# Layer 0 of a four-layer network: k's transposes into free quarters of the scores' PSUM banks, the group norm's deviation on ScalarE, two pieces of side work at other steps

## Chip, core and metric

The kernel runs on one core of one Trainium2 chip, as one launch. The metric is device time in microseconds (us), the median of several executions. Engines are named as the profile names them: PE is TensorE's matrix multiply and PEld its weight load, DVE is VectorE, ACT is ScalarE, POOL is GpSimd, SP is SyncE, which here only issues DMAs. All arithmetic is fp32.

## The reference, cut to what matters

The input x is 16 images of 192 channels on 32 by 32 pixels. Four layers follow each other, each as `x = x + layer(group_norm(x))`, and every group norm has 32 groups, so 6 channels each:

```python
def _gn(v, G=32, eps=1e-5):
    g = v.reshape(B_, G, C_ // G, H_, W_)
    m = jnp.mean(g, axis=(2, 3, 4), keepdims=True)
    s = jnp.var(g, axis=(2, 3, 4), keepdims=True)
    return ((g - m) / jnp.sqrt(s + eps)).reshape(v.shape)
```

Layer 0, where nearly all of this case happens, normalises the 1024 tokens of an image over channels, projects them to 2 x 384 (`x_in`, `z`), puts `x_in` through a causal convolution of 4 taps and a silu (`x_act`), and makes q and k from it and v from `x_in`. A recurrence with 12 heads of 32 follows:

```python
C_new = f_s * Cst + i_s * (vt[..., :, None] * kt[..., None, :])
n_new = f_s * nst + i_s * kt
h = einsum('bhde,bhe->bhd', C_new, qt) / max(abs(einsum('bhd,bhd->bh', n_new, qt)), 1)
```

Its output is normalised per head, gated, projected down and added to the tokens; a silu branch (`w_lin`) is added; a dense 3 by 3 convolution over the image and a batch norm follow. Layer 1 and layer 3 are selective scans (16 states, 384 channels), layer 2 is a depthwise convolution with batch norm.

## The kernel before, in words

**Order.** The program is written as Python generators whose instructions a scheduler then puts in an order for each engine, once, before the launch. On the chip each engine runs its own list strictly in that order. So an instruction that waits holds up everything behind it on its engine. In layer 0 the products of the recurrence are also tied to each other in a fixed order on PE (`self.main`, a chain of order-only dependencies), and the other products fall between them.

**Layer 0.** The tokens are worked on in chunks of 128, so 8 chunks to an image and 128 in all (`layer0_step`, one step per chunk). The recurrence is done chunk-wise, as in linear attention. For chunk g one step does this:

- The e tile (128 x 12 x 128: the log weights between two tokens of the chunk, per head) comes by a DMA that spreads a row over all partitions (L700). POOL adds the mask and the second gate term to it (L705, L706; both over 128 x 1536), ACT takes the exponential (L711). There are two e tiles.
- PE makes the scores, 12 products of q and k (L722), into four PSUM tiles called s, one bank each. Each uses 3 x 128 of the bank's 512 columns.
- PE transposes the chunk of k (three products, L727) into a PSUM tile called mm and DVE copies it out as kt (L728). PE transposes the chunk of v (L733) into another mm, and ACT copies it out (L736).
- DVE multiplies scores by e into four tiles p (L753; three buffers for four tiles, so the fourth waits for the first product that uses the first). PE multiplies p by v (num, L779). PE adds what comes through the state (L767) and makes the new state from kt and vr (L806; vr is made by POOL, L755).
- The output of the chunk before is normalised (L827 to L841), transposed by PE into another mm (L851) and gated (L854, L857).

[...] four for s, one for the convolution (`conv`), one for `num`, and **two for mm**. All short-lived products of layer 0, those of the recurrence as well as those of the side work, take turns in these two mm tiles. A product that needs an mm tile waits on PE until an earlier one has been read out.

**Side work of layer 0.** A small scheduler in Python (`Side`) hands out the side work by step numbers with a start and an end. Four kinds are there: the image norm of the next image (`layer0_image`), the front of the next half image (`layer0_front`: layer norm, projections, convolution, silu, q, k, gates; 12 tiles of 512 tokens in some 2.7 steps), the spread of a finished image into the tiles ya and yb by way of DRAM (`layer0_spread`, L499 to L504), and the 3 by 3 convolution in three parts of 15 or 30 products (`layer0_conv2`, L520), which ends in a copy by ACT (L526) and batch-norm statistics by DVE (L528).

**The image norm** loads the image (L539, a single buffer), takes statistics on DVE (L351, L352), averages means over the groups by a product (L355), takes the deviation of the means (L357 to L362), averages that by a second product (L365), and needs 1/sqrt of it. Before, DVE adds eps (L367) and POOL raises to the power -0.5 (L309, `pow_mhalf`). DVE then scales the image (L543), and the front's first product (L377) reads it. `group_norm` is also used 48 times in layers 1, 2 and 3.

The layers 1 and 3 are scans. PE turns B x into place (L994, L997), ACT makes the decays (L986), DVE scans (L1010), POOL multiplies by C (L1017), PE sums the states (L1028).

## Time and profile before

| what | value |
|---|---|
| time before, median of 3 runs | 17368.59 us (17350.56 to 17390.61) |
| the profiled execution: its time, its span | 17403.5 us, 17401.7 us |
| granted TensorE clock over the span, mean | 0.951 |
| PE busy | 15749.6 us, 91% of the span |
| DVE, ACT, POOL busy | 75%, 68%, 66% |
| layer 0, from 120 to 3760 us: PE busy, granted clock | 3263.08 of 3640 us, 0.88 |
| layers 1 and 2, from 3944 to 7480 us: PE busy, granted clock | 3179.91 of 3536 us, 0.98 |
| layer 3, from 7800 to 17402 us: PE busy, granted clock | 8902.43 of 9602 us, 0.98 |

The profile is of one execution, and its span is measured from the first to the last instruction. A row of the waits names the engine, the line that waited, the line that released it, the total, the number of times and the longest. A row of the timeline gives start, length, engine, line, what is written from what, and in square brackets the idle time just before. PE shows two rows' counts for each fp32 product of the program. "PEclk" is the share of full speed that the clock of PE was granted. Where a wait has several causes the profile names the one that came last.

### The profile page before, as it was taken

The numbers are of one execution on the slowest core, as the hardware profiler recorded it, in microseconds if no ns is written. First come the engines' busy times: TensorE is split into PE (matmuls) and PEld (weight loads), VectorE is DVE, ScalarE is ACT, GpSimd is POOL, SyncE is SP. The second block draws the span as 40 slices with busy tenths as digits, with TensorE's granted clock in tenths as the row PEclk, the third lists the DMA queues.
The fourth block names the chain that finished last, engine by engine and source line by source line (L and its number), as shares of the span: only waits on it lengthen the run. The fifth ranks groups of instructions, "written<-read, shape, count | busy, mean of one in ns | idle before, by whom it ended". The sixth has DMA issues, their size and how long they took to land. (4 is left out here: it accounts for less than half of the span.)

```text
span 17401.7 us, 263068 instructions
## 1 busy us (share of the span) xinstructions
PE 15749.6 (91%) x99452; PEld 11013.2 (63%) x99452; DVE 13122.0 (75%) x14859; ACT 11873.6 (68%) x19637; POOL 11450.8 (66%) x5555
## 2 busy tenths in 40 slices
PE   8998988888988899979899999999999999999998
PEld 4444444435555555547777777777777777777777
DVE  4444444437777777749889888888888888888888
ACT  3222322327666666648888888888888888888888
POOL 3333333425555555538788788888878888888888
PEclk8889998989999999989999999999999999999999
DMA  1111111123333343433333333323333333333332
GB/s 51 42 40 44 44 43 44 47 63 107 114 110 110 113 118 116 118 99 103 90 99 107 93 96 101 107 83 99 107 98 92 99 108 88 96 105 102 88 98 67
DMA packets 890141, 1544.65 MB, mean 89 GB/s; under 512 B 83472, under 2 KB 314653, under 8 KB 879530
## 3 DMA queue, kind: packets, MB, share of 16 engines
q1 hardware_dynamic: 888874, 1527.81, 30.3%
q8 instruction: 788, 12.91, 0.3%
q14 instruction: 479, 3.92, 0.1%
HBM read 1284.22 MB, written 243.27 MB: 88 GB/s over the span
## 5 line engine op out<-in xcount | busy, mean ns | idle before, releaser
L1017 POOL TENSOR_TENSOR h<-h,cb 128x1536 f32<-128x1536 f32 x2560 | 8872.8, 3469 | 1432.0 <-DVE h L1010 902.9
L986 ACT ACTIVATE da<-dt,neg_a 128x512 f32<-128x512 f32 x7680 | 5267.0, 714 | 1752.0 <-DVE h L1010 1687.3
L1010 DVE TENSOR_TENSOR_SCAN h<-da,carry,xb 128x512 f32<-128x512 f32 x3840 | 4652.4, 1262 | 657.1 <-PE xb L997 596.2
L1028 PE MATMUL y<-const,h 128*128 128x128 f32 x30720 | 4717.9, 276 | 128.3 <-DVE ysum L1468 54.0
L1010 DVE TENSOR_TENSOR_SCAN h<-da,xb 128x512 f32<-128x512 f32 x3840 | 4440.6, 1202 | 388.7 <-PE xb L997 270.7
L994 PE MATMUL xb<-const,xbt 128*128 128x128 f32 x23040 | 4074.6, 282 | 422.5 <-DVE h L1010 269.3
L966 ACT ACTIVATE xbt<-ut,bt 128x384 f32<-128x384 f32 x7680 | 4174.4, 603 | 246.4 <-PE xb L994 244.3
L994 PEld LDWEIGHTS xb<-const,xbt 128*128 128x128 f32 x23040 | 2757.2, 143 | 1815.5 <-issue 643.8
L1028 PEld LDWEIGHTS y<-const,h 128*128 128x128 f32 x30720 | 3684.9, 143 | 322.8 <-issue 265.4
L997 PE MATMUL xb<-diag,ut 128*128 128x128 f32 x15360 | 3016.4, 279 | 0.0
L997 PEld LDWEIGHTS xb<-diag,ut 128*128 128x128 f32 x15360 | 2383.5, 195 | 63.1 <-issue 63.1
L830 POOL TENSOR_TENSOR hs<-h,mhm 128x384 f32<-128x384 f32 x128 | 108.5, 848 | 1685.1 <-DVE den L835 1290.5
L1016 POOL COPY carry<-h 128x3 f32<-128x3 f32 x1280 | 250.5, 196 | 1220.1 <-DVE h L1010 964.7
L976 POOL TENSOR_TENSOR diag<-const,bt 128x512 f32<-128x512 f32 x640 | 680.8, 1064 | 550.5 <-PE xb L997 362.1
L705 POOL TENSOR_TENSOR e<-e,const 128x1536 f32<-128x1536 f32 x128 | 439.9, 3437 | 288.9 <-DMA e<-row 273.0
L520 PE MATMUL conv<-ya,w_conv 128*64 128x512 f32 (+1 forms) x1152 | 543.9, 656 | 66.1 <-DMA ya<-yrows 62.2
L916 PE MATMUL mm<-dbl,w_dt 45*128 45x512 f32 x960 | 532.8, 639 | 33.6 <-DVE v L1490 16.2
L711 ACT ACTIVATE e<-e 128x1536 f32<-128x1536 f32 x128 | 189.7, 1482 | 417.7 <-POOL e L706 417.4
L854 DVE TENSOR_TENSOR ht<-sz,mm 128x384 f32<-128x384 f32 x128 | 70.7, 552 | 519.5 <-PE mm L851 519.5
L1171 PE MATMUL mm<-rep,t_dw 96*32 96x512 f32 x2304 | 433.5, 614 | 23.5 <-DMA rep<-xr 17.3
L779 PEld LDWEIGHTS num<-v,p 128*128 128x128 f32 x3072 | 389.3, 201 | 102.2 <-issue 77.9
L920 DVE SCALAR_TENSOR_TENSOR dt<-lnsq,mm 128x512 f32<-128x512 f32 x480 | 322.0, 671 | 171.9 <-ACT lnsq L919 171.9
(272 smaller groups left out, 17910.1 us busy)
## 6 DMA issues: line engine op xcount, KB each, us to landing
cb<-row SPq DMA_DIRECT2D x2560, 256.0 KB
rep<-xr SPq DMA_DIRECT2D x384, 331.0 KB
e<-row SPq DMA_DIRECT2D x128, 768.0 KB
rep<-xin SPq DMA_DIRECT2D x384, 256.0 KB
rep<-xr SPq DMA_DIRECT2D x384, 228.8 KB
x<-x SPq DMA_DIRECT2D x48, 768.0 KB
xr<-xin SPq DMA_DIRECT2D x48, 612.5 KB
xr<-xpad SPq DMA_DIRECT2D x32, 867.0 KB
```

What stands on the lines that cost most here:

```text
L520: nc.tensor.matmul(o, self.w_c2[:k, t, c0 : c0 + o.shape[0]], src[:k, r0 : r0 + 16, dx : dx + W], start=t == 0, stop=t == 14, skip_group_c ...
L705: nc.gpsimd.tensor_tensor(k.e, k.e, self.k0("mask")[:, None, :].to_broadcast([128, NH, 128]), ADD)
L916: nc.tensor.matmul(ps, w_dt[:, t * 128 : (t + 1) * 128], dbl, start=True, stop=True)
L966: nc.scalar.activation(t[:, c], u.ut[:, c], AF.Copy, scale=u.bt[:, c, n : n + 1])
L976: nc.gpsimd.tensor_tensor(d, ident[:, None, :].to_broadcast([128, 4, 128]), u.bt[:, 3, n : n + 4][:, :, None].to_broadcast([128, 4, 128]), ...
L986: nc.scalar.activation(da[i, t], u.dt[:, t], AF.Exp, scale=u.neg_a(t, n))
L994: in_order(nc.tensor.transpose(xb[i, t][:, c * 128 : (c + 1) * 128], xbt[i][:, c, t * 128 : (t + 1) * 128], ident))
L997: in_order(nc.tensor.matmul(xb[i, t][:, 384:], u.ut[:, 3, t * 128 : (t + 1) * 128], u.diag[n // 4][:, n % 4], start=True, stop=True, skip_ ...
L1010: nc.vector.tensor_tensor_scan(hv, dv, xv, 0.0 if first else u.carry_in[:, n, t : t + 1], MUL, ADD)
L1017: nc.gpsimd.tensor_tensor(h[i], h[i], u.c.pop(n)[:, None, :].to_broadcast([128, 3, 512]), MUL)
L1028: in_order(nc.tensor.matmul(u.y[:, j], h[i][:, t, c * 128 : (c + 1) * 128], ident, is_transpose=True, start=n == 0 and j % 4 == 0, stop=n ...
L1171: self.nc.tensor.matmul(ps[32 * g : 32 * g + 32], blocks[:, g * side + r], seen, start=r == 0, stop=r == side - 1, skip_group_check=True,)
```

## The change

- `group_norm`: eps is added and the power -0.5 is taken as `exp(-0.5 * ln(v + eps))` by two instructions of ACT. The instruction of DVE (L367) and that of POOL (L309) go. This holds for all 64 group norms.
- `layer0_scores`: the four s tiles become one tile of four banks with one buffer. The three transposes of k go to the fourth quarters of banks 0, 1 and 2 and no longer to an mm tile. One copy by DVE takes the three quarters out. The products, their number and shapes are the same.
- `layer0`: the image norm starts 1.1 steps earlier and ends 0.6 steps earlier; the convolution's parts start 0.3, 0.2 and 0.1 steps later, and end at the same step.

```diff
@@ group_norm
         r = pool.tile([HP, 2], F32, name="gnr")
-        nc.vector.tensor_scalar(r, ps[:HP, :2], EPS, None, ADD)
-        self.pow_mhalf(r)
+        nc.scalar.activation(r, ps[:HP, :2], AF.Ln, bias=self.k("eps", HP))
+        nc.scalar.activation(r, r, AF.Exp, scale=-0.5)
@@ layer0
             for b in range(1, self.nb):
-                side.add("image", self.layer0_image(b, sp, bp, psum), 8 * b - 5.1, 8 * b - 4)
+                side.add("image", self.layer0_image(b, sp, bp, psum), 8 * b - 6.2, 8 * b - 4.6)
...
                 for j in range(3):
-                    at = 8 * b + 9.6 + 2.4 * j
-                    side.add("conv", self.layer0_conv2(b, j, bp, psum), at, at + 2.4)
+                    at = 8 * b + 9.9 + 2.3 * j
+                    side.add("conv", self.layer0_conv2(b, j, bp, psum), at, at + 2.3)
@@ layer0_scores
-        k.s = [psum.tile([128, 3, 128], F32, name="s", bufs=4) for _ in range(4)]
+
+        banks = psum.tile([128, 4, 4, 128], F32, name="s", bufs=1)
+        k.s = [banks[:, j, :3] for j in range(4)]
...
         k.kt = bp.tile([128, DI], F32, name="kt")
-        ps = psum.tile([128, 512], F32, name="mm")
-        for t in range(3):
-            self.main(nc.tensor.transpose(ps[:, t * 128 : (t + 1) * 128], k_[:, t, k.tok], self.k("ident")))
-        nc.vector.tensor_copy(k.kt, ps[:, :DI])
+        for t in range(3):
+            self.main(nc.tensor.transpose(banks[:, t, 3], k_[:, t, k.tok], self.k("ident")))
+        nc.vector.tensor_copy(k.kt.rearrange("p (t d) -> p t d", t=3), banks[:, :3, 3])
```

## The prediction

> **What bounds the kernel now.** I read the busy slices first, then a table by stage, then PE's waits in layer 0, then the timeline around one image norm.

> ```profile
> 120.00:3760.00 3640.00, 3263.08 (x14031) 1656.52 (x14032) 1750.30 (x3516) 1071.99 (x1604) 1405.29 (x867) 0.88 0.17 43
> ```

> Columns: PE, PEld, DVE, ACT, POOL busy, then PE's clock. In layer 0 PE is busy for 3263 of 3640 us and no other engine reaches half. PE bounds it, with 377 us idle and a clock of 0.88. Layer 3 has 93% of PE at clock 0.98. The idle time by cause, same stretch (total, times, longest):

> ```profile
> PE mm L377 <- DVE x L543: 94.9, 14, 7.6
> PE mm L851 <- ACT v L736: 65.3, 23, 4.9
> PE conv L520 <- DMA ya<-yrows: 55.4, 15, 4.9
> PE mm L851 <- DVE kt L728: 44.5, 28, 3.5
> PE mm L733 <- DVE k L613: 19.4, 16, 2.1
> PE mm L607 <- ACT v L736: 16.0, 15, 1.3
> PE mm L365 <- ACT v L736: 15.2, 13, 1.6
> PE mm L733 <- DVE xn L389: 12.6, 19, 2.2
> PE mm L569 <- DVE kt L728: 12.5, 18, 1.3
> ```

> Three causes: the front waits for the normalised image (first row), the convolution for its tile (third), and all others for one of the two mm tiles. The timeline of one image norm:

> ```profile
> 2010.57 0.35 SPq L539 DMA_DIRECT2D x<-x  x1
> ...
> 2052.70 0.25 PE L355 MATMUL mm<-gnmv,const 96*96 96x2 f32 x2
> ...
> 2058.36 0.33 PE L365 MATMUL mm<-gnq,const 96*96 96x2 f32 x2 [1.61 <-ACT v L736]
> ...
> 2059.72 0.90 PE L851 MATMUL mm<-const,hs 128*128 128x128 f32 x3 [1.04 <-DVE kt L728]
> ...
> 2063.33 2.75 POOL L706 TENSOR_TENSOR e<-e,uw 128x1536 f32<-128x1536 f32 x1
> 2066.03 0.69 POOL L309 TENSOR_TENSOR gnr<-gnr,const 96x2 f32<-96x2 f32 x1
> ...
> 2069.90 3.73 PE L377 MATMUL mm<-x,const 96*96 96x512 f32 x4 [7.27 <-DVE x L543]
> ```

> The image is there at 2011, but its first product runs at 2052.70. The power then stands on POOL behind L705 and L706, until 2066, and PE stops for 7.27 us. This chunk loses 1.61 + 1.04 + 7.27 = 9.9 us.

> [...] L309 begins as L706 ends. [...] the trace has 1283 ns (L596, L598). [...] The trace shows clock 0.70 in the image chunk (2055.20 to 2083.90) against 0.92 in 2000 to 2044.

> **The change, part by part** (line numbers of before). I use the issue order that each program was built with.

> *Image norm and deviation.* SP's order around L539 is the same in both, and L539 already waits for POOL's L600 (the single image buffer), so the load comes no earlier. What moves is the rest. L355 now stands among k's projections, before the v transposes of chunk 3 (of 8), and L365 after that chunk's L851. ACT's Ln and Exp and DVE's L543 follow: a whole chunk before L377. The image's wait of 6.8 us (94.9/14) is gone with some 10 us to spare, and POOL loses 0.69 us per image.

> What is late next? In the image chunk DVE's order is now three of p, L854, L528, L379 twice, the fourth p, and L528 waits for ACT's L526, which stands behind the exponential of the *next* e (L711), hence behind POOL. POOL's L705 starts at 2059.83 (its row came by DMA), then L841 0.83, then L706 2.75: to 66.9; L711 1.48: 68.4; L526 0.67; L528 0.68; L379 1.28; p 0.55: about 71.6. The same work before:

> ```profile
> 2067.50 0.67 ACT L526 ACTIVATE y<-conv,p 128x512 f32<-128x512 f32 x1
> ...
> 2070.49 0.68 DVE L528 BATCH_NORM_STATS2 stats_a<-y 128x6 f32<-128x512 f32 x1
> ...
> 2077.06 0.56 DVE L753 TENSOR_TENSOR p<-s,e 128x384 f32<-128x384 f32 x1
> ...
> 2079.14 0.75 PE L779 MATMUL num<-v,p 128*128 128x33 f32 x6
> ```

> PE needs the fourth p (L753 here) for the last three num products. Before, these ran at 2079.14 with 9.9 us of stops; without stops PE would be there at 2069.2. So PE stops for about 2.4 us instead of 9.9: **7.5 us per image, 15 images: -113 us.** The next e row is fetched when p frees its tile, so the later chain shifts along.

> *k's transposes out of the mm tiles.* L851 no longer takes kt's tile. Of the 44.5 us of L851 behind L728, about 15 were counted above (1.04 per image), so **-29**. L569 behind kt, 12.5: **-7**, since it inherits part of the wait for xn. L733 waits 19.4 + 12.6 (+5.4 for L811) for a tile read out late; v now takes an older one. I take half: **-17**. The products cost the same (L727 has 304 ns, as the neighbours). The copy by DVE reads three runs in three banks: nearest row L854, also rearranged, 0.552 us against L728's 0.548. Its bounds are no change and twice that; DVE is 48% busy, and the copy now stands ahead of the p's, so even double is hidden except at the fourth p. [...] One tile of four banks is freed by the last reader, not one by one. That is the fourth p, which PE's chain needs ahead of the next scores anyhow: nothing.

> *What stays.* After an image, L851 of chunk 5 waits about 3.9 us for v, whose copy stands behind the next exponential on ACT. In the new order it still does so in 13 of 16 cases. The larger part of the 65.3 us stays: it gets 1 us longer as one convolution product ahead of it is gone, and 1.4 us shorter as POOL's chain is nearer. I take **-8**.

> *New small waits.* One convolution product no longer stands between chunk 6's v and q's projections (L607, which wait for v's copy): +1.0 x 16 = **+16**. L355 between k's projections takes a tile and makes the third projection wait for DVE's second read: about 1 x 14 = **+14**. ACT gets Ln and Exp, nearest rows L839 and L840 at 0.21 us; queued where ACT is mostly idle (busy 1.95 of 11 us, 2044 to 2055): nothing. Table loads: one more in the whole program, +1.3, before the first image.

> *Convolution.* In the built order the first product of an image (L520) stands where it stood, right behind v's transposes of chunk 2 and ahead of L607. The spread is unchanged on SP. So the 55.4 us **stay**; if the move worked they would go, the bound below. The other parts start about a dozen products later, as filler: nothing by themselves.

> *Clock.* L377 has 899 ns over its 120 rows where L589, of the same size, has 612: 34 us in the stage lost to the halved clock. With the stop before it gone I take about half, **-18**. Bounds: nothing, and -90 (a fifth of the 0.12 x 3640 = 437 us that the clock costs).

> *Layers 1 to 3.* In layer 3 PE's order is the same; in layers 1 and 2, 732 of 3474 products other than the scan's changed place by a few. PE's stops at the norm are 28.7 us (L377 behind L1240), 72.4 (L355 behind its statistics, which stays). DVE waits 23.7 us for POOL's power in layer 3, off PE's path. I take **-10**, between -60 and +60.

> Sum: -113 - 29 - 7 - 17 - 8 + 16 + 14 + 1 - 18 - 10 = **-171 us**. The profiled execution took 17403.5 and would come to 17232. It is 35 us above the median of the runs, 17368.6, which would come to **17198**.

> **The rivals.**

> *The fourth p gives half back* (0.20). If POOL's chain in the image chunk ends 4 us later than I worked out (the e row lands later, or DVE's L543, 0.8 to 4.7 us long, delays L694 and with it L706), the image is worth 3.5 us, not 7.5: 60 less, about 17260; up to 17330 if kt's waits return as well. For it: three engines in a row stand behind one DMA. Against: only L841 is put into that chain.

> *The clock recovers* (0.13): up to 90 instead of 18, or the convolution's 55 go too: 17060 to 17140. Against: a chunk that makes no image norm and idles 0.3 us (2172 to 2199) has clock 0.81, so short products alone lower it.

> *Nothing comes of it* (0.06): the stops move to other mm users, tile for tile, as the rows of L851 allow: 17334 to 17403.

> *The clock falls* (0.09, slower): convolution products, the long ones, leave the stretches between short products, and the halved clock spreads. Stage at 0.88 loses 437 us. To end 35 us slower it must lose 171 + 35 more, 643 of about 3675: clock 0.825. Below that point it decides; price about 17420. For it: 0.81 exists in this stage (2172 to 2199). Against: the number of long products per chunk changes by one or two[...].

> **How the numbers follow.** Likeliest, 17140 to 17250: 0.52. With the give-back, and most of the clock's recovery, 17100 to 17330 holds 8 in 10. A difference of 0.2%, 35 us, is about what a measurement of this kernel can tell. Faster by more: 0.52 + 0.20 + 0.13 = 0.85; within: 0.06; slower: 0.09.

> **What would show it.** Right: L377 behind L543 gone from PE's waits; L851 behind L728 gone; L520 behind ya still near 55; a new stop at num for p of 2 to 3 us per image; L607 behind v near 30; PE's idle time in layer 0 about 230 us instead of 377, the stage some 160 shorter; layers 1 to 3 within 60 us. Wrong: a stop of over 6 us at num per image (give-back), a clock in layer 0 under 0.85 (slower), or a difference that lies in layers 1 to 3.

## The result, and the profile after

The changed kernel takes **17154.22 us**, median of 4 runs (17148.25 to 17170.01), against 17367.28 us of the kernel before in the same comparison (17350.56 to 17390.61): a ratio of **0.9878, 95% interval 0.9861 to 0.9895**, 213 us less. On a second chip it was 17137.39 against 17360.18, 0.9875 (0.9859 to 0.9892). The prediction said 17198, between 17100 and 17330. The time is in the range. But only about a quarter of the gain is idle time of PE in layer 0, where the prediction looked for nearly all of it; the experiments below show where the rest came from.

The profiled execution took 17158.12 us, its span is 17156.3 us at a mean clock of 0.959 (before 0.951). Layer 0 ends some 190 us earlier: the first scan of layer 1 starts at 3755.3 us, before at 3943.8. Lines up to L717 keep their numbers; the scores, L722, are L724, and from L727 on every line is one higher (L736 is L737, L851 is L852).

The table by stage, for layer 0 of the kernel after, has the columns shown before the change (PE, PEld, DVE, ACT, POOL busy, then PE's clock):

```profile
120.00:3570.00 3450.00, 3127.78 (x14038) 1632.15 (x14039) 1751.20 (x3502) 1077.39 (x1638) 1403.58 (x852) 0.92 0.18 45
```

PE still idles 322 of 3450 us. That is 55 less than before, where the prediction expected some 147 less. The clock went from 0.88 to 0.92. PE's waits in layer 0 (total, times, longest):

```profile
PE mm L852 <- ACT v L737: 86.8, 24, 6.4
PE conv L520 <- DMA ya<-yrows: 61.2, 16, 6.4
PE conv L520 <- ACT y L526: 36.7, 12, 6.2
PE mm L569 <- DVE xn L389: 20.3, 13, 2.7
PE mm L607 <- ACT v L737: 18.1, 15, 1.3
PE num L780 <- DVE p L754: 17.2, 17, 2.2
...
PE mm L355 <- DVE k L613: 10.1, 13, 0.8
```

The rows of L377 behind L543 and of L851 behind kt are gone, as forecast, and the stop behind ya stayed. But L852 behind v grew from 65.3 to 86.8 us, and the row of the convolution that waits for its own bank until ACT has read it (L526) grew from 2.4 to 36.7. The timeline of one image norm shows both halves, the gain and the new stop:

```profile
1944.42 0.25 PE L365 MATMUL mm<-gnq,const 96*96 96x2 f32 x2
...
1944.72 0.26 ACT L367 ACTIVATE gnr<-mm,const 96x2 f32<-96x2 f32 x1 [0.62 <-PE mm L365]
...
1945.44 4.65 DVE L543 TENSOR_SCALAR x<-x,gnmean,gnr 96x1024 f32<-96x1024 f32 x2
...
1961.49 3.44 POOL L705 TENSOR_TENSOR e<-e,const 128x1536 f32<-128x1536 f32 x1 [2.50 <-ACT v L737]
...
1961.68 1.96 PE L377 MATMUL mm<-x,const 96*96 96x512 f32 x4
...
1969.85 0.67 ACT L526 ACTIVATE y<-conv,p 128x512 f32<-128x512 f32 x1
...
1970.57 2.07 PE L520 MATMUL conv<-ya,w_conv 128*128 128x512 f32 x2 [4.33 <-ACT y L526]
...
1972.35 0.55 DVE L754 TENSOR_TENSOR p<-s,e 128x384 f32<-128x384 f32 x1
...
1972.95 1.49 PE L780 MATMUL num<-v,p 128*128 128x33 f32 x6 [0.30 <-DVE p L754]
```

The deviation is ready at 1945, a chunk early, and L377 runs without a stop. The chain behind POOL's L705 takes what the prediction worked out: the fourth p starts 10.9 us after it (forecast 11.2, from 2059.83 to 2071.0). But PE is there sooner than forecast. The clock is full until 1967.24, so that L377 takes 1.96 us and not the 3.73 of before, and PE stops for 4.33 + 0.30 us instead of the predicted 2.4. One convolution product stands just ahead of the last num products and needs the bank that L526 reads. L526 is a link of that same chain, so most of the stop shows in its row and not at num.

In layers 1 to 3, between the first scan and the end, the trace has 13,401 us instead of 13,458. The wait that became shorter is this one, before and after:

```profile
PE xb L994 <- DVE h L1010: 269.3, 254, 3.8
```

```profile
PE xb L995 <- DVE h L1011: 219.9, 235, 3.5
```

### The profile page after: what moved, and what is told of

Same layout as the page of the kernel before. It is cut to its first block, busy times and chain, and to the rows that moved or that the text cites. A ratio compares the mean times of both kernels' runs of the same rounds, so it can differ in the third digit from the quotient of the medians.

```text
span 17156.3 us, 262939 instructions
## 1 busy us (share of the span) xinstructions
PE 15613.4 (91%) x99452; PEld 10979.0 (64%) x99452; DVE 13102.8 (76%) x14795; ACT 11895.7 (69%) x19766; POOL 11422.4 (67%) x5491
## 5 line engine op out<-in xcount | busy, mean ns | idle before, releaser
L705 POOL TENSOR_TENSOR e<-e,const 128x1536 f32<-128x1536 f32 x128 | 443.3, 3464 | 244.0 <-DMA e<-row 226.9
L520 PE MATMUL conv<-ya,w_conv 128*64 128x512 f32 (+1 forms) x1152 | 500.9, 646 | 99.4 <-DMA ya<-yrows 61.2
L711 ACT ACTIVATE e<-e 128x1536 f32<-128x1536 f32 x128 | 189.7, 1482 | 445.6 <-POOL e L706 445.6
L1172 PE MATMUL mm<-rep,taps 128*32 128x512 f32 x3072 | 423.8, 607 | 27.9 <-DMA rep<-xr 17.8
```

The lines of the kernel that those rows point to most:

```text
L520: nc.tensor.matmul(o, self.w_c2[:k, t, c0 : c0 + o.shape[0]], src[:k, r0 : r0 + 16, dx : dx + W], start=t == 0, stop=t == 14, skip_group_c ...
L705: nc.gpsimd.tensor_tensor(k.e, k.e, self.k0("mask")[:, None, :].to_broadcast([128, NH, 128]), ADD)
L1172: self.nc.tensor.matmul(ps[32 * g : 32 * g + 32], blocks[:, g * side + r], seen, start=r == 0, stop=r == side - 1, skip_group_check=True,)
```

## The experiments

All kernels at a glance. "Ratio" is to the kernel before on the same chip. "Idle" is PE's idle time in layer 0, from 120 us to 190 us before the first scan; "halved" is how long PE was busy at the halved clock (0.50 in the clock's records) in that stretch, both added up from one trace each. (A chunk's time at the halved clock, below, and the halved times in the expectations count PE's idle time too.) "First scan" is where layer 1's first scan starts. A chunk's length, below, runs from its v transposes on PE to those of the next, as a mean over the 16 images.

| kernel | ratio (95%) | idle us | halved us | first scan us |
|---|---|---|---|---|
| before | 1 | 377 | 698 | 3943.8 |
| after | 0.9878 (0.9861 to 0.9895) | 322 | 488 | 3755.3 |
| after_again | 0.9875 (0.9859 to 0.9892) | 314 | 472 | 3735.8 |
| o_gn | 0.9949 (0.9935 to 0.9964) | 316 | 705 | 3884.9 |
| o_banks | 0.9955 (0.9939 to 0.9972) | 377 | 468 | 3808.5 |
| o_image | 1.0007 (0.9998 to 1.0015) | 308 | 812 | 3931.5 |
| o_conv | 0.9955 (0.9940 to 0.9970) | 326 | 580 | 3827.6 |
| gi | 1.0005 (0.9996 to 1.0013) | 318 | 893 | 3981.3 |
| u_image | 0.9881 (0.9866 to 0.9896) | 301 | 516 | 3747.4 |
| u_conv | 0.9965 (0.9952 to 0.9977) | 339 | 697 | 3888.8 |
| all_d | 0.9863 (0.9848 to 0.9878) | 275 | 514 | 3731.8 |
| all_v | 0.9847 (0.9833 to 0.9862) | 304 | 406 | 3700.5 |
| all_vcx | 0.9840 (0.9825 to 0.9854) | 300 | 416 | 3693.6 |

If an instruction of PE takes twice as long at the halved clock (as L377 above, 3.73 us for 1.96), half of its time there is lost, and layer 0 should end earlier by the idle time lost plus half of the halved time lost. For o_gn that gives 61 - 3 = 58 (measured 59), for o_image 69 - 57 = 12 (12), for o_conv 51 + 59 = 110 (116), for gi 59 - 97 = -38 (-37.5). For these four the account closes. For o_banks it gives 115 of 135 and for the kernel after 160 of 188.5: where k's transposes stand in the banks, 16 to 32 us more come off. They lie mainly on the convolution's products and v's transposes, and no run explains them.

One profile of a kernel is not its median: the first scan of the two profiles of the changed kernel differs by 20 us. The profile of the kernel before is 35 us above its median, so differences to its row come out some tens of us larger than those of the medians: o_image's profile is 50 us shorter, its median is not.

The first theory, the prediction's, is that time goes where PE's waits go ("wait theory"). Its rival is that the time follows the granted clock, that is, which products stand where ("clock theory").

**o_gn: the deviation on ScalarE alone.**

```diff
-        nc.vector.tensor_scalar(r, ps[:HP, :2], EPS, None, ADD)
-        self.pow_mhalf(r)
+        nc.scalar.activation(r, ps[:HP, :2], AF.Ln, bias=self.k("eps", HP))
+        nc.scalar.activation(r, r, AF.Exp, scale=-0.5)
```

> The kernel before with one edit: the group norm's power on ScalarE; banks and steps as before. Theory of waits (the prediction's): the image norm keeps its place, but no longer stands behind POOL's two additions, so of the 94.9 us that L377 waits for the image about 20 to 30 stay (Ln and Exp stand behind L839 and L840 on ACT, to about 2061, and L543 takes up to 4 us). Layer 0 is 75 us shorter: the first scan of layer 1 starts near 3870 us instead of 3943.8, the whole near 17290. Rival, the clock: the gain in the changed kernel came mainly from the halved clock of TensorE in chunks 0 and 4 of each image, which this part hardly touches; then chunk 4 gets its 5 us, chunk 0 stays at 27 us, and the clock of layer 0 stays at 0.88 to 0.89.

Measured: 17264.09 us against 17346.58, 82 less.

```profile
PE mm L377 <- DVE x L543: 51.6, 15, 4.9
```

The wait went from 94.9 to 51.6 and the clock stayed. Here the wait theory is right: 61 us of idle time went, and the first scan comes 59 us earlier, where it expected 75. The rest is not in layer 0. Over all traces, the stretch from the first scan to the end is 13,379 to 13,401 us in the nine kernels with the deviation on ScalarE and 13,420 to 13,458 in the four without (PE's wait for the scan there is 214 to 225 us in the nine, 256 to 268 in the four): some 50 us of this edit are won in layers 1 to 3.

**o_banks: k's transposes in the scores' banks alone.**

```diff
-            self.main(nc.tensor.transpose(ps[:, t * 128 : (t + 1) * 128], k_[:, t, k.tok], self.k("ident")))
+            self.main(nc.tensor.transpose(banks[:, t, 3], k_[:, t, k.tok], self.k("ident")))
```

> The kernel before with one edit: k's transposes in the free quarters of the scores' banks. Theory of waits: L851 and L569 behind kt (44.5 and 12.5 us) go, L733 behind k and xn halves, L607 behind v gains 16; L377 still ends at the image norm, so what chunk 4 saves ahead of it is lost again. Layer 0 about 35 us shorter, first scan near 3909, the whole near 17330. Rival, the clock: chunk 0 of each image is 6.6 us shorter in the changed kernel with only 1.5 us of it idle time; if this part does it (its L851 no longer stops in chunk 0), layer 0 is 100 us or more shorter, first scan near 3840, and the clock of layer 0 rises to 0.90.

Measured: 17264.93 us, 82 less.

```profile
PE mm L851 <- ACT v L736: 97.3, 26, 5.7
PE mm L377 <- ACT y L526: 84.9, 13, 8.4
```

The waits for kt are gone and these two took their place: idle 377 before, 377 here. What the account explains of the gain is all clock. Chunk 0 of an image goes from 27.0 to 20.5 us, of which 15.4 and 5.1 at the halved clock. The wait theory falls for this part. In the fifth image PE's order of products in this chunk is the same in both kernels, and only the stops differ. By the count in the last section (columns times share of rows in windows of 3.41 us, with a limit near 1550 that was read from these traces) the chunk lies close to the limit: four windows at the halved clock have 1190, 1300, 1150 and 1490 before, and the clock stays down; in o_banks the first one has 1620, and the clock comes back.

**o_image: the image norm's steps alone.**

```diff
-                side.add("image", self.layer0_image(b, sp, bp, psum), 8 * b - 5.1, 8 * b - 4)
+                side.add("image", self.layer0_image(b, sp, bp, psum), 8 * b - 6.2, 8 * b - 4.6)
```

> The kernel before with one edit: the image norm's steps (8b - 6.2 to 8b - 4.6). Theory of waits: L355 and L365 stand a chunk earlier, the power on POOL has a chunk to spare, L377 behind L543 goes from 94.9 us to under 10, and L365's 20 us go. Chunk 4 is 7 to 8 us shorter per image: layer 0 about 105 us shorter, first scan near 3840, the whole near 17260. Rival (give-back): the stop moves to num for the fourth p, behind L528 and L526 on DVE and ACT, and only half, 50 us, comes.

Measured: 17355.66 us, no difference that can be measured.

```profile
120.00:3740.00 3620.00, 3312.31 (x13972) 1696.45 (x13972) 1712.09 (x3502) 1072.05 (x1603) 1403.55 (x865) 0.88 0.17 43
```

L377 behind L543 is gone and 69 us of idle time with it. PE is busy 59 us longer instead (3253.08 us before, to 3750): more of the work runs at the halved clock, 812 us for 698. Compare o_conv.

**o_conv: the convolution's steps alone.**

```diff
-                    at = 8 * b + 9.6 + 2.4 * j
+                    at = 8 * b + 9.9 + 2.3 * j
```

> The kernel before with one edit: the convolution's steps (9.9 and 2.3). Theory of waits: the first product of an image keeps its place behind v's transposes of chunk 2, so the 55 us behind the ya tile stay and nothing is gained: first scan within 15 us of 3943.8, the whole within 35 us of 17367. Rival, the clock: two convolution products more stand ahead of L377 in chunk 0 and the other products are spread otherwise; if that is what raised the clock in chunk 0 from 15 to 5 us halved, layer 0 is 60 to 80 us shorter although no wait goes.

Measured: 17270.68 us, 76 less.

```profile
120.00:3640.00 3520.00, 3194.05 (x14036) 1640.17 (x14035) 1720.58 (x3515) 1071.34 (x1608) 1409.49 (x866) 0.90 0.18 44
```

The edit that the prediction priced at nothing is worth as much as the others. The stop behind ya is there (51.3 us). In the built order about two of an image's 60 convolution products move from chunk 2 to chunk 1 and one more stands in chunk 3. o_image and o_conv take about the same idle time away (69 and 51 us); one spreads the halved clock by 114 us, the other shortens it by 118. That is the difference between nothing and 76 us. Why this order keeps the clock up chunk by chunk was not taken further.

**gi: deviation and image norm together,** the step with the highest price in the prediction.

```diff
-        self.pow_mhalf(r)
+        nc.scalar.activation(r, r, AF.Exp, scale=-0.5)
...
+                side.add("image", self.layer0_image(b, sp, bp, psum), 8 * b - 6.2, 8 * b - 4.6)
```

> The kernel before with the group norm's deviation by ScalarE and the image norm at its new steps, and nothing else: the step that the prediction priced highest. Prediction's own terms (-113 for the image, +14 for L355, +1): ratio 0.994, 98 us faster. The two runs of the parts alone, added: 0.9956, 76 us. Clock theory: the idle time of layer 0 falls by 60 to 100 us, but the time at the halved clock stays at the 840 us of before or rises as with the image's steps alone, so 30 to 80 us faster: 0.9955 to 0.998.

Measured: 17355.15 us against 17342.84, no difference. Both expectations missed; the clock theory had the sign of the clock right, not its size.

```profile
PE mm L767 <- ACT gnr L367: 47.7, 13, 4.0
```

The stop at L377 became a stop at L767, half a chunk earlier, and PE was busy at the halved clock for 195 us longer. What it gains in layers 1 to 3 it loses in layer 0.

**u_conv: the changed kernel with the convolution's old steps.**

```diff
-                    at = 8 * b + 9.9 + 2.3 * j
+                    at = 8 * b + 9.6 + 2.4 * j
```

> The changed kernel with the convolution back at its old steps. Prediction's reading: the stop behind ya stays either way and L607 behind v gains 16 us back: the same as the changed kernel to 16 us faster, 0.986 to 0.9875. Clock theory: the long products go back from chunks 0 and 4 to where they were; the halved time of chunk 0 rises from 5 us per image to 8 or more and that of chunk 4 by some 5: 40 to 80 us slower, 0.990 to 0.992.

Measured: 17279.39 us, 0.9965, outside both expectations: 148 us slower than u_image on the same chip, which is as fast as the changed kernel. The waits have this row:

```profile
PE mm L767 <- ACT gnr L367: 63.9, 13, 5.3
```

And its timeline, in chunk 3 of an image:

```profile
1997.48 0.33 PE L365 MATMUL mm<-gnq,const 96*96 96x2 f32 x2 [0.27 <-ACT v L736]
...
2001.45 3.41 POOL L622 TENSOR_TENSOR xact<-xact,sz 128x1536 f32<-128x1536 f32 x1
...
2004.90 1.95 ACT L625 ACTIVATE sz<-sz,p 128x512 f32<-128x512 f32 x3 [7.47 <-POOL xact L622]
...
2006.75 0.24 ACT L367 ACTIVATE gnr<-mm,const 96x2 f32<-96x2 f32 x1
...
2007.05 1.69 PE L767 MATMUL mm<-state,q 128*128 128x132 f32 x6 [5.11 <-ACT gnr L367]
```

L365's product is done at 1997.8, but its reader, the logarithm L367, stands on ACT behind three L625, which wait for POOL's L622, which stands behind L705. L767 needs the mm tile that L367 reads: 5.11 us. In the kernel after, ACT has L367 and L368 *ahead of* the L625 (1944.72 above; L625 follows at 1953.42). Around L365 the two programs differ by one convolution product, which stands before or behind it, and the scheduler put L367 and the three L625 on ACT the other way round. The same order stands in gi. The kernel after has it too, for one image of 14: there chunk 3 takes 27.7 us, for the other 13 images 15.2 to 19.2. Chunk 3 takes 24.1 us here, 13.9 of them halved, against 17.6 and 4.4 after: (24.1 - 17.6) x 16 = 104 us of the 133 by which the first scan is later. So here a wait and the clock go together, and the traces point to the order on ACT as what starts it; no run turned that order alone.

**u_image: the changed kernel with the image norm's old steps.**

```diff
-                side.add("image", self.layer0_image(b, sp, bp, psum), 8 * b - 6.2, 8 * b - 4.6)
+                side.add("image", self.layer0_image(b, sp, bp, psum), 8 * b - 5.1, 8 * b - 4)
```

> The changed kernel with the image norm back at its old steps (8b-5.1 to 8b-4). Prediction's reading: L377 waits again for the image, without POOL's power some 3.4 us per image as with the deviation on ScalarE alone, so 35 to 60 us slower than the changed kernel: 0.990 to 0.991. Clock theory: the image's steps were worth nothing by themselves, because the stops went and the halved clock spread; so within 25 us of the changed kernel, 0.986 to 0.989.

Measured: 17131.07 us, 0.9881, within the interval of the kernel after, as the clock theory had it.

```profile
120.00:3560.00 3440.00, 3139.39 (x14022) 1633.48 (x14022) 1754.29 (x3497) 1079.39 (x1638) 1405.99 (x851) 0.91 0.18 46
```

The image norm's new steps bring nothing measurable, alone or beside the others. The medians of the four parts alone add up to 231 us, near the 213 of all together, but the parts don't simply add: two of them together (gi) give nothing, and all but the convolution's steps (u_conv) give 63.

**after_again: the changed kernel on the chip of the next three.**

There is no edit; it is the base for them.

> The changed kernel once more, on the same chip as the three below, as the base they are compared with. Expected: ratio to before 0.986 to 0.990. A second profile of it tells how far one profile of a kernel can be trusted: PE's idle time from 120 to 3600 us within 10 us of 329, time at the halved clock within 40 us of 594.

Measured: 17137.39 us, idle and halved time as in the first profile.

**all_d: work added where PE stood.**

```diff
+        if k.g % 8 == 5:
+            for _ in range(8):
+                self.main(nc.tensor.transpose(banks[:, 3, 3], k_[:, 0, k.tok], self.k("ident")))
```

> The changed kernel with work added: eight more transposes of 128 columns in chunk 5 of each image, right behind v's three, into the free quarter of the fourth score bank; nothing reads them. They stand ahead of L852, which in 13 of 16 images waits 5.2 us for v's copy. Wait theory: eight of 0.3 us fit into the stop, the copy comes when it came, and in the three images without a stop 2.4 us are added: +7 us against the changed kernel, within 15. Clock theory: PE streams columns where it stood, so fewer windows fall under some 1600 columns; chunk 5 at the halved clock falls from 6.9 us per image to 3 or less, its length from 37.9 to about 36, and the kernel gets 25 to 50 us faster although it does more.

Measured: 17125.15 us. That is 12 less than after_again with overlapping intervals: not to be told from no change.

```profile
PE mm L854 <- ACT v L739: 62.8, 21, 5.8
```

This row had 81.8 us in after_again. 128 added transposes cost nothing that can be measured; chunk 5 at the halved clock fell from 7.3 to 4.8 us per image, its length from 38.0 to 37.0, but over the layer PE was busy at the halved clock 42 us longer, part of it with the added work. The clock theory's 25 to 50 us did not come. The run fits the wait theory's "within 15" as well.

**all_v: v's copy ahead of the next exponential on ACT.**

```diff
+            self.tc.add_manual_dep(ins.ins, self.v_copy, why)
```

Here `ins` is the exponential L711 and `v_copy` the copy L737 of the chunk before, tied in order only.

> The changed kernel, with v's copy by ACT (L737) put ahead of the next chunk's exponential in the 27 chunks where it stood behind it; nothing else moves on PE. Wait theory: L852 behind L737 goes from 86.8 us to under 15 and L607 behind it from 18 to some 10; the exponential comes 0.5 us later where it was first, which p does not feel: 75 us less idle, so 65 to 85 us faster than the changed kernel. Clock theory: the same and, since the stops before short products go, another 30 to 60 from the clock: 95 to 140 us. If neither holds and the stop goes on to the next product that takes an mm tile, under 30.

Measured: 17092.37 us, 45 less than after_again and less than either theory said; its slowest run is below the fastest of after_again.

```profile
PE mm L569 <- ACT xin L571: 77.8, 28, 5.6
```

L852 behind v is gone. L569, the next user of an mm tile, now waits instead (11.1 us in after_again): its tile is read by L571, and that stands behind the exponential too. Idle fell by 10 us only; halved time fell by 66. The third case in the expectation, a stop that goes on to the next user, held for the waits.

**all_vcx: the same, and the convolution later.**

```diff
-                    at = 8 * b + 9.9 + 2.3 * j
+                    at = 8 * b + 10.4 + 2.15 * j
...
+                if t == 0 and part == 0:
+                    self.tc.add_manual_dep(mm.ins, self.main.last, why)
```

> As the one before, and the convolution later: its parts start at steps 8b+10.4, 12.55 and 14.7, and the first product of each image is tied behind the recurrence's product that was issued last at that point, so that it stands some 60 products later, behind q's and k's projections of chunk 2. Wait theory: L520 behind ya (61 us) goes, L520 behind L526 (37 us) goes, since the second part begins a chunk later: 150 to 180 us faster than the changed kernel. Clock theory: less, or even nothing beyond the one before: chunks 2 and 3 lose long products to later chunks, chunk 2 then has only 128- and 33-column products beside the projections, and its halved time (under 8 us now) rises by 5 us or more per image.

Measured: 17082.09 us, the **fastest of all**; its interval (0.9825 to 0.9854) lies below that of after_again. The stops behind ya and L526 went, but only 10 us come on top of all_v, and the runs of the two overlap.

```profile
PE mm L773 <- ACT gnr L367: 69.5, 14, 6.7
```

L367 stands behind the three sz activations of ACT again (L625, here L628), so chunk 3 is as in u_conv (24.4 us, 13.1 halved). A version with L367 held ahead of L625 was not tried.

**clock_probe: products that wait for nothing.**

```diff
+            for count, n in ((300, 512), (300, 128), (600, 33), (300, 128), (100, 512), (200, 64), (100, 256), (200, 96)):
+                for _ in range(count):
+                    tc.nc.tensor.matmul(ps[:, :n], self.k("ident"), z[:, :n], start=True, stop=True)
```

> The changed kernel with a stream of products ahead of layer 0 that wait for nothing and that nothing uses: 300 of 512 columns, 300 of 128, 600 of 33, 300 of 128, 100 of 512, 200 of 64, 100 of 256, 200 of 96. Only the granted clock within each group counts here, not the time of the whole. If the clock falls only where PE stands idle, it is full in all eight groups. If it goes by the columns that PE streams in a window of 3.41 us, as layer 0's windows read (halved under some 1600, restored above some 2000): full for 512, 256 and 128 columns (0.3 us each, 2900 columns a window, each product counted for its two records), halved throughout the 600 of 33 columns (some 700 to 1000 a window even at full clock), and restored in the second group of 128 within one or two windows or not at all, since at the halved clock a full window of these just reaches 2000; halved in the groups of 64 columns, and near the edge in the group of 96.

Measured, a stretch inside each of the groups of 512, 128, 33, again 128, and 64 columns (PE busy, PEld busy, ..., clock):

```profile
30.00:280.00 250.00, 250.00 (x580) 110.60 (x579) 1.41 (x4) 0.00 (x0) 0.00 (x0) 1.00 0.00 0
295.00:350.00 55.00, 55.00 (x495) 55.00 (x494) 0.00 (x0) 0.00 (x0) 0.00 (x0) 1.00 0.00 1
365.00:600.00 235.00, 235.00 (x1104) 235.00 (x1103) 0.00 (x0) 0.00 (x0) 0.00 (x0) 0.50 0.00 1
612.00:670.00 58.00, 58.00 (x521) 58.00 (x521) 0.00 (x0) 0.00 (x0) 0.00 (x0) 1.00 0.00 1
...
762.00:802.00 40.00, 40.00 (x360) 40.00 (x360) 0.00 (x0) 0.00 (x0) 0.00 (x0) 1.00 0.01 1
```

PE is busy for every one of these microseconds by its records, and the clock is 0.50 for the 33 columns and 1.00 for the others: full to 350 us, halved from 365 to 600, full again from 612. All groups stream zeros, so only the width differs. In this probe, then, idle time is not what the clock goes by. The expectation was wrong for 64 columns, which stay at full clock.

## Why the prediction was right or wrong

- **Right in what it said of single rows.** L377 behind L543 gone, L851 behind kt gone, ya's stop still there (61.2 for 55.4), the third projection behind L355 (10.1 us for 14), a stop at num for p in the image's chunk (about 1 us each; the rest of it shows behind L526).
- **The image norm, -113: the step failed.** In the program as a whole chunk 4, where the image norm stood, idles 3.3 us instead of 8.9, as a mean over the 15 images, so 84 us less rather than 113. The 9.9 us of the image shown were above the mean, and "without stops PE would be there at 2069.2" kept the halved clock's durations; at full clock PE reaches the fourth p earlier and waits longer than 2.4 us. And the sum took what chunk 4 loses as the worth of the edit: the two edits together give nothing (gi), where the stop at L377 became one at L767 and the halved time rose by 195 us, and without the new steps the changed kernel is as fast (u_image).
- **k's transposes, -29 -7 -17, and v, -8: mechanism wrong.** The waits for kt went, and the idle time did not change (o_banks); it passed to the next users of the mm tiles. The rival "stops move tile for tile" described the waits better, and was wrong on the time, because the clock rose (halved time 698 to 468 us). For v, 21 us more instead of 8 less.
- **L607 behind v, +16:** 2 us (16.0 to 18.1).
- **Convolution, 0: the step failed.** "As filler: nothing by themselves" looked at PE alone. Alone the edit is worth 76 us; within the change some 150, by the traces for the larger part because it keeps L367 ahead of L625 on ACT. The prediction looked at ACT's order only in the one program, where it is the good one, and so put the gain down to other edits.
- **Clock, -18 with bounds 0 and -90: mis-sized.** PE was busy at the halved clock 210 us less (698 to 488), worth 105 us if half of it is lost; that is outside the bound. The reason it gave, fewer stops, isn't enough: o_image has 69 us less idle time and more halved time. The rival that the clock recovers, with its chance of 0.13, named nearly the size, not a cause; the rival that the clock falls had one that fits the counts in the last section, long products leaving the stretches between short ones.
- **Layers 1 to 3, -10 between -60 and +60:** about -50, from the deviation off POOL and DVE. The bound held, the value was low.

The profile became 245 us shorter, 74 more than the forecast 171: the waits were overrated by some 90 us, the clock and layers 1 to 3 underrated by some 130, and some 30 are in no term. The medians differ by 213 us only, since the profile of the kernel before was itself 35 us above its median. That the time came out 44 us from the forecast, inside the range, is in part luck: errors of opposite sign took most of each other away.

## What to carry to other kernels

Where a few tiles are shared by many products, removing a wait can hand it to the next user of a tile (o_banks, all_v): count the idle time of the engine, not the row that is gone. Price a moved instruction on every engine whose order it can change, since one product's place decided whether a 0.24 us instruction stood behind a 3.4 us one of another engine (u_conv). And keep an account of the time at the halved clock beside that of the idle time, chunk by chunk; here it was the larger of the two.

## What the runs showed of the hardware

  | window, by this count | before | after |
  |---|---|---|
  | full clock, under 1550 | 72 of 74 | 79 of 83 |
  | full clock, over 1550 | 7 of 737 | 5 of 754 |
  | halved clock, under 1550 | 160 of 165 | 84 of 86 |
  | halved clock, over 1550 | 12 of 87 | 3 of 85 |

  Over layer 0 of the 13 kernels' traces this limit is wrong for 217 of 13,337 windows; in layers 1 to 3, from which it was not taken, for 165 of 51,022 (10 of 3942 before, 13 of 3926 after). The count and its limit describe these traces: no run varied the rows alone, and none shows what the chip itself counts.
- In layer 0 most windows that lost the clock hold a stop as well: of the 74 under 1550 in the kernel before, PE is busy for over 95% of the time in 16 only. By this count a long product in the right chunk would keep the clock up, and so would the end of a stop; neither was shown by itself, since the experiments with the order moved both at once.
- In the probe the two-record fp32 product has a floor: 128, 96 and 64 columns all take 0.11 us per record (521 in 58 us, 361 and 360 in 40 us), and PE's weight load is busy all that time. From 128 down to 64 columns nothing was saved, and PE streamed half as many columns in a window (1970 for 3920).
- In these traces an instruction that waits holds up those behind it on its engine. In the kernel before, POOL's L309 starts at 2066.03 us, as L706 ends (2063.33 and 2.75 long). In u_conv ACT's logarithm of 0.24 us stands behind three L625, and PE waits 5.11 us for it.
- A table load on ACT took 1283 ns each time, 227 times in the kernel before and 228 times in the kernel after.
